# A decoder's two LSTMs: gate sums in three PSUM tiles, half steps written out by hand, and inputs added as three bf16 numbers

## The chip, the core and the metric

The kernel runs on one core of one Trainium2 chip. The metric is the device time of one launch in microseconds (us); lower is better. TensorE is called PE, VectorE DVE, ScalarE ACT, GpSimd POOL and SyncE SP, as the profile does.

## The reference, cut to what matters

The reference is a decoder of four layers with three sublayers each, over 8 sequences of 112 tokens of width 256. The change touches one part of the first sublayer only: the two LSTMs that make its queries and keys. Everything else of the decoder is the same in both kernels.

```python
xW = jnp.einsum('bsd,gd->sbg', x, Wih) + b          # inputs, all steps at once
def step(carry, xt):
    h, c = carry
    gates = xt + h @ Whh.T                          # 8 x 1024, h is 8 x 256
    i, f, g, o = jnp.split(gates, 4, axis=-1)
    c = sigmoid(f) * c + sigmoid(i) * tanh(g)
    h = sigmoid(o) * tanh(c)
    return ((h, c), h)
hq = _lstm(hidden_states, Wih_q, Whh_q, b_q)        # 112 steps
hk = _lstm(hidden_states, Wih_k, Whh_k, b_k)        # 112 steps, independent of hq
```

Each LSTM is a chain of 112 steps in which a step needs the `h` of the step before. The two LSTMs (called chain 0 and chain 1 below) do not need each other. All arithmetic is float32.

## The kernel before, in words

`l0_attn` normalises and transposes the tokens (`ln_T_mm`), runs `lstm`, projects the values (`vv`, line 553) and then attends (`l0_attend`). `xs` keeps the transposed tokens for the LSTMs; it is grouped so that 16 steps of 8 sequences (a block `m` of 128 tokens, seven blocks in all) lie together.

**Layout of a step.** The 1024 gate sums of a chain are spread over four groups `j` of 256 columns, and group `j` is written to PSUM partitions 32j to 32j+31, of which 8 (the sequences) carry numbers. So one tile `g` of 128 x 256 holds all gates of one step, in the order i, f, o, g, 64 columns each, and every ACT and DVE operation on the gates works on 128 partitions.

**PE work of a step.** `from_inputs` (line 609) starts the sums of a step: four matmuls, one for each `j`, whose stationary operand `pick` chooses the 8 rows of step `t` out of the block's 128 rows of `xw`. The recurrent product (line 631) adds `h @ Whh`: two halves `c` of the hidden state by four `j`, 8 matmuls of 256 columns, with the transposed state `hT` (128 x 32, of which 8 columns carry numbers) as the stationary operand. A float32 matmul appears in the trace as two records, and as two weight loads.

**ACT and DVE work of a step.** A sigmoid over 192 columns (line 642), a tanh over 64 (line 643), then on DVE c·f, i·g and their sum (lines 648, 650, 651), tanh of the cell on ACT (line 653), `h` on DVE (line 655), and DVE's transposition in blocks of 32 x 32 into `hT` (line 657). POOL copies `hT` to `hs` for the attention (line 658).

**Inputs.** `inputs` (lines 597 to 604) projects one block of 16 steps for one chain and 512 of its columns: two float32 matmuls of 512 columns with 128 x 128 weights, and a bias add on DVE that writes `xw`. Four such calls stand ahead of the first step; the other 24 are made one after every fourth step (`if t % 4 == 2 and later`).

**What sets the order.** Both chains are written in one loop over `t`, chain 0 and then chain 1. Nothing in the order is by hand: a scheduler orders each engine's instructions, and each engine runs its own in order. The tiles `g0`, `g1` have two PSUM buffers each.

Of the kernel before, what the change touches and what calls it, by code (L numbers as in the profile page):

```python
# [90 lines left out]
def _gates(w):  # L91

    i, f, g, o = np.split(w, 4, axis=0)
    a = np.stack([i, f, o, g]).reshape(4, 2, 4, 32, *w.shape[1:])
    return np.moveaxis(a, 2, 0).reshape(1024, *w.shape[1:])


# [155 lines left out]
def _constants():  # L253

    f32 = np.float32
    i = np.arange(S)
    le = (i[:, None] <= i[None, :]).astype(f32)
    d = i[:, None] - i[None, :]
    k = np.where(np.abs(d) <= 3, np.exp(-(d.astype(f32) ** 2) / f32(2.0 * 0.4**2)), 0).astype(f32)
    local = k / (k.sum(axis=-1, keepdims=True) + f32(1e-10))  # L260
    inv = (1.0 / 10000.0 ** (np.arange(0, 128, 2, dtype=f32) / f32(128))).astype(f32)
    ang = np.outer(inv, i.astype(f32)).astype(f32)
    cos, sin = np.cos(ang), np.sin(ang)

    pick = np.zeros((P, 16, 32), f32)
    for r in range(16):
        pick[16 * np.arange(8) + r, r, np.arange(8)] = 1

    sums = (np.arange(P)[:, None] == 32 * np.arange(4)[None, :] + 16).astype(f32)
    return [  # L270
        ("ident", np.eye(P, dtype=f32)),
        ("causal", np.where(le.T > 0, f32(0), f32(NEG))),
        ("le", le),
        ("gt", 1 - le),
        ("localT", f32(1.0 - 0.6) * local.T),
        ("cos", np.concatenate([cos, cos])),
        ("sin", np.concatenate([sin, -sin])),
        ("ones", np.ones((S, S), f32)),
        ("pick", pick.reshape(P, 512)),
        ("sums", sums),  # L280
        ("first", np.broadcast_to(np.arange(8, 0, -1, dtype=f32)[None], (P, 8))),
    ]
# [65 lines left out]
class _Kernel:  # L348
# [187 lines left out]
    def l0_attn(self):  # L536
        nc, tc, w = self.nc, self.tc, self.w
        with ExitStack() as outer:
            keep = outer.enter_context(tc.tile_pool(name="l0a", bufs=1))
            hs = self.t(keep, [P, S, 2, 2, NB], "hs")  # L540
            vv = self.t(keep, [P, NB, 4, 65], "vv")
            with tc.tile_pool(name="ps_l0a", bufs=2, space=PSUM) as ps:
                xs = self.t(keep, [P, 2, S // 16, NB, 16], "xs")
# [12 lines left out]
            self.l0_attend(hs, vv)  # L556
        w.done("l0a_bv")

    def ln_T_mm(self, ps, xs):

        self.normalise(self.x, self.xn)
        for half in range(2):
            for kc in range(2):
                tp = self.t(ps, [P, 512], "mm")
                for j in range(HB):
                    self.nc.tensor.transpose(
                        tp[:, j * S : (j + 1) * S],
                        self.xn[:S, half * HB + j, kc * P : (kc + 1) * P],
                        self.ident[:S, :S],
                    )  # L570
                bs = slice(half * HB, (half + 1) * HB)
                self.nc.vector.tensor_copy(
                    xs[:, kc, :, bs, :].rearrange("p m b r -> p b m r"),
                    tp[:, :HT].rearrange("p (b m r) -> p b m r", b=HB, r=16),
                )
                self.nc.scalar.copy(self.xnT[:, kc, half * HT : (half + 1) * HT], tp[:, :HT])

    def lstm(self, hs, xs, ps0):
# [4 lines left out]

        nc, tc = self.nc, self.tc
        G = range(4)
        whh = [self.w("l0a_hh_q", 2), self.w("l0a_hh_k", 2)]
        wih = [self.w("l0a_ih_q", 2), self.w("l0a_ih_k", 2)]
        bias = [self.w("l0a_b_q"), self.w("l0a_b_k")]  # L590
        pick = self.c("pick").rearrange("p (r m) -> p r m", r=16)
        with tc.tile_pool(name="ps_lstm", bufs=2, space=PSUM) as ps, tc.tile_pool(
            name="lstm", bufs=2
        ) as work, tc.tile_pool(name="lstm_c", bufs=1) as cpool:

            xw = self.t(cpool, [P, 2, S // 16, 1024], "xw")
            cell = [self.t(cpool, [P, 64], f"cell{l}") for l in range(2)]

            def inputs(m, l, half):
                cols = slice(512 * half, 512 * half + 512)  # L600
                pm = self.t(ps0, [P, 512], "mm")
                steps = [xs[:, k, m, :, :].rearrange("p b r -> p (b r)") for k in range(2)]
                self.mm(pm, [(x, wih[l][:, k, cols]) for k, x in enumerate(steps)])
                nc.vector.tensor_tensor(xw[:, l, m, cols], pm, bias[l][:, cols], ALU.add)

            def from_inputs(t, l):
                g = self.t(ps, [P, 256], f"g{l}")
                for j in G:
                    nc.tensor.matmul(  # L609
                        g[32 * j : 32 * j + 32, :],  # L610
                        pick[:, t % 16, :],
                        xw[:, l, t // 16, 256 * j : 256 * j + 256],
                        start=True,
                        stop=t == 0,
                        skip_group_check=True,
                    )
                return g

            for l in range(2):
                for half in range(2):  # L620
                    inputs(0, l, half)
            later = [(m, l, half) for m in range(1, S // 16) for l in range(2) for half in range(2)]
            gs = [from_inputs(0, l) for l in range(2)]
            hT = [None, None]
            for t in range(S):
                for l in range(2):
                    g = gs[l]
                    if t > 0:
                        for c in range(2):
                            for j in G:  # L630
                                nc.tensor.matmul(  # L631
                                    g[32 * j : 32 * j + 32, :],
                                    hT[l][:, c, :],
                                    whh[l][:, c, 256 * j : 256 * j + 256],
                                    start=False,
                                    stop=c == 1,
                                    skip_group_check=True,
                                )
                    if t + 1 < S:
                        gs[l] = from_inputs(t + 1, l)  # L640
                    sg = self.t(work, [P, 256], f"sg{l}")
                    nc.scalar.activation(sg[:, :192], g[:, :192], AF.Sigmoid)  # L642
                    nc.scalar.activation(sg[:, 192:], g[:, 192:], AF.Tanh)
                    ig, fg, og, gg = (sg[:, 64 * i : 64 * i + 64] for i in range(4))
                    if t == 0:
                        nc.vector.tensor_tensor(cell[l], ig, gg, ALU.mult)
                    else:
                        nc.vector.tensor_tensor(cell[l], cell[l], fg, ALU.mult)
                        tmp = self.t(work, [P, 64], f"tmp{l}")
                        nc.vector.tensor_tensor(tmp, ig, gg, ALU.mult)  # L650
                        nc.vector.tensor_tensor(cell[l], cell[l], tmp, ALU.add)  # L651
                    th = self.t(work, [P, 64], f"th{l}")
                    nc.scalar.activation(th, cell[l], AF.Tanh)  # L653
                    h = self.t(work, [P, 64], f"h{l}")
                    nc.vector.tensor_tensor(h, og, th, ALU.mult)  # L655
                    hT[l] = self.t(work, [P, 2, 32], f"hT{l}")
                    nc.vector.transpose(hT[l].rearrange("p c b -> p (c b)"), h)  # L657
                    nc.gpsimd.tensor_copy(hs[:, t, l, :, :], hT[l][:, :, :NB])
                if t % 4 == 2 and later:
                    inputs(*later.pop(0))  # L660

    def l0_attend(self, hs, vv):
        nc, tc, w = self.nc, self.tc, self.w
# [1374 lines left out]
```

## Time and profile before

| what | value |
|---|---|
| median of 3 runs (lowest, highest) | 2502.42 us (2501.94, 2503.11) |
| the profiled execution, its own time | 2510.28 us |
| its span in the profile | 2508.5 us |
| mean granted PE clock | 0.93 of full |
| granted PE clock from 20 to 430 us | 1.00 |
| busy over the span: PE, DVE, ACT, POOL | 88%, 58%, 32%, 8% |
| LSTM part in the trace: first `from_inputs`, last `hT` written | 31.45 us, 433.07 us |
| start of the last recurrent product | 429.58 us |

The profiled execution took 7.9 us more than the median of the timed runs; durations below are from it. A line such as `L631 PE MATMUL g<-w,hT 128*32 128x256 f32 x3552 | 237.5, 384` reads: line 631, matmuls with a 128 x 32 stationary operand and a 128 x 256 moving one, 3552 records, busy 237.5 us in all (overlaps counted once), 384 ns for one from start to modelled end. After the second bar stands the idle time before them and what ended it.

### The profile page before, as it was taken

What the parts mean: (1) busy time and instruction counts of PE and PEld (TensorE: products, weight loads), DVE (VectorE), ACT (ScalarE), POOL (GpSimd) and SP (SyncE); (2) the same over time, 40 slices, a digit from 0 to 9 for tenths busy, and PEclk for the clock granted to TensorE, in tenths of its full rate; (3) what the DMA queues carried; (4) which work ended last, traced back from release to release, by engine and by line L of the source; (5) the groups of instructions that cost most, each with busy time, mean ns of one, the idle gap of its engine ahead of it and who ended that gap; (6) DMA issues with size and microseconds to landing.
All of it is one profiled execution on the core that took longest, in us unless ns stands there. A gap on an engine that the chain in (4) does not pass through costs nothing.

```text
span 2508.5 us, 43456 instructions
## 1 busy us (share of the span) xinstructions
PE 2219.0 (88%) x17256; PEld 1347.1 (54%) x17256; DVE 1464.2 (58%) x3879; ACT 795.9 (32%) x1988; POOL 212.8 (8%) x416
## 2 busy tenths in 40 slices
PE   6999999989989889999998887899999999799942
PEld 3444444657655656655666444556555556556622
DVE  4565656555544657763688555767660042667698
ACT  2333333111221245641012222367521111346521
POOL 0111111000001110000111331100000000100000
PEclk9999999786899999999999988899999999799966
DMA  4000001000010000001000001000111000000000
GB/s 182 2 2 2 2 19 61 1 17 1 17 51 1 14 18 2 18 18 42 34 3 35 15 18 59 34 2 1 51 51 50 33 17 1 1 1 2 2 0 15
DMA packets 10730, 56.15 MB, mean 22 GB/s; under 512 B 1833, under 2 KB 3625, under 8 KB 5792
## 3 DMA queue, kind: packets, MB, share of 16 engines
q1 hardware_dynamic: 8304, 44.77, 4.9%
q0 software_dynamic: 2080, 7.07, 0.8%
q8 instruction: 137, 2.24, 0.4%
q10 hardware_dynamic: 144, 1.54, 0.2%
q14 instruction: 65, 0.53, 0.1%
HBM read 52.43 MB, written 0.92 MB: 21 GB/s over the span
## 4 chain that ended last, share of the span: by engine, by line
PE 68%; DVE 21%; issue 5%; ACT 4%; DMA 1%; POOL 1%; DVEq 0%; ACTq 0%; POOLq 0%
PE mm L397 32%; PE tr L1058 6%; PE gu L397 6%; PE g L631 6%; PE sc L397 5%; PE av L1074 3%; PE av L397 3%; DVE rot L1367 1%; ACT sg L642 1%; PE s L397 1%; ACT th L653 1%; DVE hT L657 1%; PE g L609 1%; PE tr L397 1%; DVE h L655 1%
## 5 line engine op out<-in xcount | busy, mean ns | idle before, releaser
L631 PE MATMUL g<-w,hT 128*32 128x256 f32 x3552 | 237.5, 384 | 25.7 <-DVE hT L657 24.4
L397 PE MATMUL mm<-xnT,w 128*128 128x448 f32 x432 | 185.8, 567 | 19.4 <-DVE qT L1370 4.5
L1058 PEld LDWEIGHTS tr<-cst,xe 112*125 112x125 f32 x1152 | 151.3, 188 | 96.2 <-issue 36.9
L1045 DVE TENSOR_REDUCE xnm<-sc 112x1 f32<-112x375 f32 x384 | 184.4, 541 | 28.7 <-PE sc L397 28.0
L1058 PE MATMUL tr<-cst,xe 112*125 112x112 f32 x1152 | 192.7, 289 | 8.6 <-DVE xeT L1066 3.4
L397 PE MATMUL mm<-hT,w 128*128 128x448 f32 x512 | 193.0, 540 | 0.0
L631 PEld LDWEIGHTS g<-w,hT 128*32 128x32 f32 x3552 | 96.0, 109 | 167.0 <-DVE hT L657 124.3
L397 PEld LDWEIGHTS mm<-hT,w 128*128 128x128 f32 x512 | 97.3, 190 | 94.2 <-issue 94.2
L397 PE MATMUL mm<-w,oT 128*112 128x256 f32 x416 | 121.0, 449 | 21.6 <-DVE oT L1547 14.2
L609 PE MATMUL g<-xw,cst 128*32 128x256 f32 x1792 | 138.7, 379 | 0.0
L1066 DVE COPY xeT<-tr 125x336 f32<-125x336 f32 x192 | 97.2, 506 | 69.1 <-PE tr L1058 61.6
L397 PEld LDWEIGHTS mm<-xnT,w 128*128 128x128 f32 x432 | 79.0, 196 | 104.0 <-issue 54.0
L1064 ACT COPY xeT<-tr 125x336 f32<-125x336 f32 x192 | 85.0, 443 | 155.0 <-PE tr L1058 155.0
L397 PE MATMUL mm<-w,hT 128*112 128x256 f32 x576 | 132.3, 389 | 0.2 <-DVE xo L1638 0.2
L1049 ACT ACTIVATE xe<-sc,xnm 112x375 f32<-112x375 f32 x256 | 126.3, 582 | 9.2 <-DVE xnm L1045 9.2
L397 PE MATMUL gu<-xnT,w 128*128 128x448 f32 x320 | 124.4, 544 | 1.7 <-DVE hT L1212 1.2
L397 PEld LDWEIGHTS mm<-w,hT 128*112 128x112 f32 x576 | 103.5, 182 | 27.5 <-issue 4.9
L397 PEld LDWEIGHTS mm<-w,oT 128*112 128x112 f32 x416 | 83.9, 211 | 53.4 <-DVE oT L1547 14.4
L642 ACT ACTIVATE sg<-g 128x192 f32<-128x192 f32 x224 | 73.9, 330 | 105.3 <-PE g L631 93.9
L653 ACT ACTIVATE th<-cell 128x64 f32<-128x64 f32 x224 | 57.4, 256 | 146.8 <-DVE cell L651 146.7
L474 DVE TENSOR_TENSOR x<-mm,x 112x256 f32<-112x256 f32 x64 | 27.0, 422 | 129.8 <-PE mm L397 129.8
L655 DVE TENSOR_TENSOR h<-sg,th 128x64 f32<-128x64 f32 x224 | 50.5, 225 | 84.5 <-ACT th L653 84.5
(381 smaller groups left out, 3755.8 us busy)
## 6 DMA issues: line engine op xcount, KB each, us to landing
w<-in_w SPq DMA_DIRECT2D x33, 1024.0 KB, 4.9
w<-in_w SPq DMA_DIRECT2D x4, 896.0 KB, 11.4
raw<-in_wq POOLq DMA_DIRECT2D x3, 1024.0 KB, 5.1
wi<-in_wint POOLq DMA_DIRECT2D x3, 768.0 KB, 6.0
w<-in_w SPq DMA_DIRECT2D x2, 768.0 KB, 4.2
ctxT<-in_ctxT ACTq DMA_DIRECT2D x1, 1500.0 KB, 8.4
cx<-in_ctx POOLq DMA_DIRECT2D x1, 1500.0 KB, 21.0
w<-in_w SPq DMA_DIRECT2D x2, 512.0 KB, 4.0
```

Of the source, the lines that this page charges most:

```text
L397: self.nc.tensor.matmul(out, lhsT, rhs, start=i == 0, stop=i == len(pairs) - 1)
L609: nc.tensor.matmul(g[32 * j : 32 * j + 32, :], pick[:, t % 16, :], xw[:, l, t // 16, 256 * j : 256 * j + 256], start=True, stop=t == 0, sk ...
L631: nc.tensor.matmul(g[32 * j : 32 * j + 32, :], hT[l][:, c, :], whh[l][:, c, 256 * j : 256 * j + 256], start=False, stop=c == 1, skip_group ...
L642: nc.scalar.activation(sg[:, :192], g[:, :192], AF.Sigmoid)
L653: nc.scalar.activation(th, cell[l], AF.Tanh)
L655: nc.vector.tensor_tensor(h, og, th, ALU.mult)
L1045: nc.vector.tensor_reduce(nm, sc, AX.X, ALU.max, negate=True)
L1049: nc.scalar.activation(e, sc, AF.Exp, bias=nm)
L1058: nc.tensor.transpose(tp[:CH, i * S : (i + 1) * S], e[:, i * CH : (i + 1) * CH], self.ident[:S, :S])
L1064: nc.scalar.copy(eT, src)
L1066: nc.vector.tensor_copy(eT, src)
L1074: nc.tensor.matmul(avs[b][32 * j : 32 * j + 32, c * S : (c + 1) * S], values[b % 2][:CH, i, 4 * c + j, :], eTs[b, c, j][:, i, :], start=i ...
```

## The change

Five things change, all in `lstm` and in what prepares for it.

1. **Gates in three parts.** The gate order becomes g, i, f, o, and a step's sums lie in three PSUM tiles, `ga` (g and i, 128 columns), `gf` (64) and `go` (64), each with one buffer. Each matmul of 256 columns becomes three, of 128, 64 and 64. The activations become one tanh over 64 columns and three sigmoids over 64.
2. **Half steps.** The loop runs over 224 half steps `n` (step `n // 2` of chain `n % 2`), and the order on PE, DVE and ACT is the order of the code (`manual_schedule`). In half step `n` PE runs the recurrent product of its chain, then the other chain's `from_inputs` for half step `n + 1`. ACT runs this chain's tanh, then the other chain's tanh of its cell (`state`), then the three sigmoids.
3. **State.** The cell and the output gate are transposed on their own (`cT`, `oT`), so tanh of the cell and `hT` work on 128 x 16, and `hT` is 128 x 2 x 8: its stationary operand has 8 columns and not 32.
4. **Inputs as three bf16 numbers.** For blocks 1 to 6 a projected input is cut into three bf16 numbers whose sum it is: ACT copies to bf16 and POOL subtracts, twice, and POOL copies the rest. Twelve DMAs from SBUF to SBUF for each block and chain (144 in all, 32 partitions by 1024 columns each) bring the three numbers of a token under each other (rows 0-31, 32-63, 64-95 of `moved`). `from_inputs` then multiplies by `add3` (96 x 32, bf16), which chooses and adds the three. Block 0 stays float32.
5. **Projection 64 columns a time.** A generator, `inputs`, makes 128 columns of a block in five stages, of which one is run in each half step (two in each of the first 16): 64 columns, 64 columns and the bias add, then the three cuts. 96 such generators run; from half step 16 on a new one starts at every even `n`, the last at `n` = 174. Half steps 176 to 223 have no projection.

Two small parts: `pick` and `xs` are laid out with the step ahead of the sequence, and three DVE copies make `add3` at the start.

```diff
-    a = np.stack([i, f, o, g]).reshape(4, 2, 4, 32, *w.shape[1:])
+    a = np.stack([g, i, f, o]).reshape(4, 2, 4, 32, *w.shape[1:])
...
-        pick[16 * np.arange(8) + r, r, np.arange(8)] = 1
+        pick[8 * r + np.arange(8), r, np.arange(8)] = 1
...
+            add3 = self.t(cpool, [P, 4, 32], "add3", BF16)
+            for i in range(3):
+                nc.vector.tensor_copy(add3[32 * i : 32 * i + 32], pick[:32, :4, :])
...
+            def inputs(m, l, q):
+                cols = slice(128 * q, 128 * q + 128)
+                pm = self.t(ps0, [P, 512], "mm")[:, :128]
+                for i in range(2):
+                    projected(pm[:, 64 * i : 64 * i + 64], m, l, slice(128 * q + 64 * i, 128 * q + 64 * i + 64))
+                    if i == 0:
+                        yield
+                x = self.t(work, [P, 128], "x")
+                nc.vector.tensor_tensor(x, pm, bias[l][:, cols], ALU.add)
...
+                for i in range(3):
+                    yield
+                    part = cuts[l][:, i, cols]
+                    if i == 2:
+                        nc.gpsimd.tensor_copy(part, x)
+                    else:
+                        nc.scalar.copy(part, x)
+                        nc.gpsimd.tensor_tensor(x, x, part, ALU.subtract)
+                if q == 7:
+                    moved[m, l] = self.t(work, [P, 4, 1024], f"xm{l}", BF16)
+                    for i in range(3):
+                        for r in range(4):
+                            nc.sync.dma_start(
+                                moved[m, l][32 * i : 32 * i + 32, r, :], cuts[l][32 * r : 32 * r + 32, i, :]
+                            )
+            def product(g, lhsT, rhs, l, part, start, stop):
+                at, n = PARTS[part]
                 for j in G:
                     nc.tensor.matmul(
+                        g[32 * j : 32 * j + lhsT.shape[1], :], lhsT, rhs[:, 256 * j + at : 256 * j + at + n],
+                        start=start, stop=stop, skip_group_check=True,
                     )
...
+                    if m == 0:
+                        product(g, pick[:, r, :], first[l], l, part, True, t == 0)
+                    else:
+                        product(g, add3[:96, r % 4, :], moved[m, l][:96, r // 4, :], l, part, True, False)
...
+            def state(t, l):
+                cT, oT = turned[l]
+                th = self.t(work, [P, 2, NB], f"th{l}")
+                nc.scalar.activation(th, cT[:, :, :NB], AF.Tanh)
+                hT[l] = self.t(work, [P, 2, NB], f"hT{l}")
+                nc.vector.tensor_tensor(hT[l], oT[:, :, :NB], th, ALU.mult)
+                nc.gpsimd.tensor_copy(hs[:, t, l, :, :], hT[l])
+            with tc.manual_schedule(engines={ET.PE, ET.DVE, ET.Activation}):
+                gs = [from_inputs(0, 0), None]
+                for n in range(2 * S):
+                    t, l = n // 2, n % 2
                     if t > 0:
+                        for part, g in enumerate(gs[l]):
+                            for c in range(2):
+                                product(g, hT[l][:, c, :], whh[l][:, c, :], l, part, False, c == 1)
+                    ga, gf, go = gs[l]
+                    if n + 1 < 2 * S:
+                        gs[1 - l] = from_inputs((n + 1) // 2, 1 - l)
...
+                    nc.scalar.activation(flat[:, :64], ga[:, :64], AF.Tanh)
+                    if n > 0:
+                        state((n - 1) // 2, 1 - l)
+                    nc.scalar.activation(flat[:, 64:128], ga[:, 64:], AF.Sigmoid)
+                    tmp = self.t(work, [P, 64], f"tmp{l}") if t > 0 else cell[l]
+                    nc.vector.tensor_tensor(tmp, ig, gg, ALU.mult)
+                    nc.scalar.activation(flat[:, 128:192], gf, AF.Sigmoid)
+                    nc.scalar.activation(flat[:, 192:], go, AF.Sigmoid)
+                    if t > 0:
                         nc.vector.tensor_tensor(cell[l], cell[l], fg, ALU.mult)
                         nc.vector.tensor_tensor(cell[l], cell[l], tmp, ALU.add)
+                    turned[l] = [self.t(work, [P, 2, 32], f"{i}T{l}") for i in "co"]
+                    nc.vector.transpose(turned[l][0].rearrange("p c b -> p (c b)"), cell[l])
+                    nc.vector.transpose(turned[l][1].rearrange("p c b -> p (c b)"), og)
+                    for i in range(2 if n < 16 else 1):
+                        running = [r for r in running if next(r, r) is not r]
+                        if later and (i == 0 if n < 16 else n % 2 == 0):
+                            running.append(inputs(*later.pop(0)))
+                            next(running[-1])
+                state(S - 1, 1)
```

More of the change, by code (lines that the diff above doesn't have):

```diff
@@ L542, in l0_attn @@
             with tc.tile_pool(name="ps_l0a", bufs=2, space=PSUM) as ps:
-                xs = self.t(keep, [P, 2, S // 16, NB, 16], "xs")
+                xs = self.t(keep, [P, 2, S // 16, 16, NB], "xs")
                 self.ln_T_mm(ps, xs)
@@ L572, in ln_T_mm @@
                 self.nc.vector.tensor_copy(
-                    xs[:, kc, :, bs, :].rearrange("p m b r -> p b m r"),
+                    xs[:, kc, :, :, bs].rearrange("p m r b -> p b m r"),
                     tp[:, :HT].rearrange("p (b m r) -> p b m r", b=HB, r=16),
@@ L587, in lstm @@
         G = range(4)
+        PARTS = ((0, 128), (128, 64), (192, 64))
         whh = [self.w("l0a_hh_q", 2), self.w("l0a_hh_k", 2)]
@@ L590, in lstm @@
         bias = [self.w("l0a_b_q"), self.w("l0a_b_k")]
-        pick = self.c("pick").rearrange("p (r m) -> p r m", r=16)
-        with tc.tile_pool(name="ps_lstm", bufs=2, space=PSUM) as ps, tc.tile_pool(
+        with tc.tile_pool(name="ps_lstm", bufs=1, space=PSUM) as ps, tc.tile_pool(
             name="lstm", bufs=2
         ) as work, tc.tile_pool(name="lstm_c", bufs=1) as cpool:
-            xw = self.t(cpool, [P, 2, S // 16, 1024], "xw")
+            pick = self.c("pick").rearrange("p (r m) -> p r m", r=16)
+            add3 = self.t(cpool, [P, 4, 32], "add3", BF16)
+            for i in range(3):
+                nc.vector.tensor_copy(add3[32 * i : 32 * i + 32], pick[:32, :4, :])
@@ L597, in lstm, with projected @@
             cell = [self.t(cpool, [P, 64], f"cell{l}") for l in range(2)]
[L599 to L602, printed above, removed]
+            first = [self.t(cpool, [P, 1024], f"xw{l}") for l in range(2)]
+            cuts, moved = {}, {}
+            def projected(pm, m, l, cols):
+                steps = [xs[:, k, m, :, :].rearrange("p r b -> p (r b)") for k in range(2)]
@@ L603, in inputs @@
                 self.mm(pm, [(x, wih[l][:, k, cols]) for k, x in enumerate(steps)])
-                nc.vector.tensor_tensor(xw[:, l, m, cols], pm, bias[l][:, cols], ALU.add)
-            def from_inputs(t, l):
-                g = self.t(ps, [P, 256], f"g{l}")
+            def inputs(m, l, q):
[7 more added lines that the diff above has]
+                nc.vector.tensor_tensor(x, pm, bias[l][:, cols], ALU.add)
+                if q == 0:
+                    cuts[l] = self.t(cpool, [P, 3, 1024], f"xc{l}", BF16)
+                for i in range(3):
[13 more added lines that the diff above has]
+                            )
@@ L608, in from_inputs @@
+            def product(g, lhsT, rhs, l, part, start, stop):
+                at, n = PARTS[part]
                 for j in G:
                     nc.tensor.matmul(
[L610 to L615, printed above, removed]
-                    )
-                return g
+                        g[32 * j : 32 * j + lhsT.shape[1], :], lhsT, rhs[:, 256 * j + at : 256 * j + at + n],
+                        start=start, stop=stop, skip_group_check=True,
+                    )
@@ new lines, in from_inputs @@
+            def from_inputs(t, l):
+                gs = [self.t(ps, [P, 512], f"g{l}{part}")[:, :n] for part, (_, n) in enumerate(PARTS)]
+                m, r = t // 16, t % 16
+                for part, g in enumerate(gs):
+                    if m == 0:
+                        product(g, pick[:, r, :], first[l], l, part, True, t == 0)
+                    else:
+                        product(g, add3[:96, r % 4, :], moved[m, l][:96, r // 4, :], l, part, True, False)
+                return gs
@@ L619, in lstm @@
             for l in range(2):
                 for half in range(2):
[L621 to L627, printed above, removed]
-                    if t > 0:
[L629 to L647, printed above, removed]
@@ new lines, in lstm @@
+                    cols = slice(512 * half, 512 * half + 512)
+                    pm = self.t(ps0, [P, 512], "mm")
+                    projected(pm, 0, l, cols)
+                    nc.vector.tensor_tensor(first[l][:, cols], pm, bias[l][:, cols], ALU.add)
+            later = [(m, l, q) for m in range(1, S // 16) for l in range(2) for q in range(8)]
+            running = []
+            hT, turned = [None, None], [None, None]
+            def state(t, l):
[5 more added lines that the diff above has]
+                nc.gpsimd.tensor_copy(hs[:, t, l, :, :], hT[l])
@@ new lines, in lstm @@
+            with tc.manual_schedule(engines={ET.PE, ET.DVE, ET.Activation}):
+                gs = [from_inputs(0, 0), None]
+                for n in range(2 * S):
+                    t, l = n // 2, n % 2
+                    if t > 0:
+                        for part, g in enumerate(gs[l]):
[4 more added lines that the diff above has]
+                        gs[1 - l] = from_inputs((n + 1) // 2, 1 - l)
+                    sg = self.t(work, [P, 4, 64], f"sg{l}")
+                    flat = sg.rearrange("p g u -> p (g u)")
+                    gg, ig, fg, og = (sg[:, i, :] for i in range(4))
+                    nc.scalar.activation(flat[:, :64], ga[:, :64], AF.Tanh)
[7 more added lines that the diff above has]
+                    if t > 0:
@@ L648, in lstm @@
                         nc.vector.tensor_tensor(cell[l], cell[l], fg, ALU.mult)
-                        tmp = self.t(work, [P, 64], f"tmp{l}")
-                        nc.vector.tensor_tensor(tmp, ig, gg, ALU.mult)
                         nc.vector.tensor_tensor(cell[l], cell[l], tmp, ALU.add)
[L652 to L660, printed above, removed]
+                    turned[l] = [self.t(work, [P, 2, 32], f"{i}T{l}") for i in "co"]
+                    nc.vector.transpose(turned[l][0].rearrange("p c b -> p (c b)"), cell[l])
+                    nc.vector.transpose(turned[l][1].rearrange("p c b -> p (c b)"), og)
```

## The prediction

> **What bounds the kernel now.** I read the costliest groups first, for the share of the LSTM part, then the timeline of one step, to see what a step waits for, then the timeline around one input projection. The groups (line, engine, operation, shape, count, busy us, mean ns of one, idle before):
>
> ```profile
> L631 PE MATMUL g<-w,hT 128*32 128x256 f32 x3552 | 237.5, 384 | 25.7 <-DVE hT L657 24.4
> L609 PE MATMUL g<-xw,cst 128*32 128x256 f32 x1792 | 138.7, 379 | 0.0
> L642 ACT ACTIVATE sg<-g 128x192 f32<-128x192 f32 x224 | 73.9, 330 | 105.3 <-PE g L631 93.9
> ```
>
> PE looks full, yet it waits for `hT`, and ACT waits for PE: the two are on one chain. The timeline of 408 to 412 us (start, duration, engine, line) follows one chain through a step:
>
> ```profile
> 408.23 1.07 PE L631 MATMUL g<-w,hT 128*32 128x256 f32 x16
> ...
> 409.42 0.33 ACT L642 ACTIVATE sg<-g 128x192 f32<-128x192 f32 x1 [0.16 <-PE g L631]
> ...
> 409.93 0.22 DVE L650 TENSOR_TENSOR tmp<-sg 128x64 f32<-128x64 f32 x1
> ...
> 410.18 0.23 DVE L651 TENSOR_TENSOR cell<-cell,tmp 128x64 f32<-128x64 f32 x1
> ...
> 410.50 0.26 ACT L653 ACTIVATE th<-cell 128x64 f32<-128x64 f32 x1 [0.63 <-DVE cell L651]
> ...
> 410.79 0.23 DVE L655 TENSOR_TENSOR h<-sg,th 128x64 f32<-128x64 f32 x1 [0.38 <-ACT th L653]
> ...
> 411.45 1.07 PE L631 MATMUL g<-w,hT 128*32 128x256 f32 x16
> ```
>
> From 408.23 to 411.45 is 3.22 us, and this is the period of a step nearly everywhere: the latency of PE, ACT, DVE, ACT, DVE in turn, 1.61 us for each half step. PE's own work is less. Sixteen records of 384 ns end within 1.07 us because the four column groups run side by side: records start 6 to 7 ns apart in fours, and fours follow each other by 216 ns. So a product costs 4 x 0.216 = 0.86 us of PE, `from_inputs` 0.43, both chains 2.6 us of 3.22. Every fourth step a projection comes in:
>
> ```profile
> 199.54 0.62 PE L609 MATMUL g<-xw,cst 128*32 128x256 f32 x8
> ...
> 200.09 1.98 PE L397 MATMUL mm<-w,xs 128*128 128x512 f32 x4
> ...
> 202.00 0.59 PEld L631 LDWEIGHTS g<-w,hT 128*32 128x32 f32 x16 [0.76 <-DVE hT L657]
> ```
>
> That step takes 4.80 us, 1.58 more: 24 x 1.58 = 38 us. 112 x 3.22 + 38 = 399 us, and the trace has 401.6 from the first `from_inputs` to the last `hT`.
>
> **What the Trainium skill says.** TensorEngine Tiling (Array Packing), Key Properties: a change of tiling mode drains TensorE. The trace agrees: the last four of L609 start at 199.78 and stream 0.213, the 128-column weights load at 200.09; the last L397 starts at 201.48 and streams 0.427, the next load is at 202.00. Both gaps are 0.095 us. TensorE: Matmul & The Clock Gate, LDWEIGHTS: a load takes its columns over 1.2 GHz; here 128-column float32 loads follow each other by 0.107 us, and at 112 columns short matmuls (65 columns wide) come every 0.098: the load bounds them. Its section Back-to-back issue gap has a floor of about 25 ns between matmuls; between column groups this trace has 6 to 7. SBUF — State Buffer, section SBUF: two separate sides: GpSimd and a VectorE operation with two SBUF inputs exclude each other. The trace agrees: line 1410 on DVE takes 407 ns alone and 941 beside POOL.
>
> **The change, part by part.** The changed program's order on PE is as written: 24 matmuls of the product, 12 of the other chain's `from_inputs`, then the projection's two.
>
> *Product.* Per 4 groups, 4 rounds of 128 columns and 8 of 64. By the width (216 ns for 256, 95.5 for 112 in the `av` matmuls of line 1074, also with 32-column loads) a round of 128 is 0.109, one of 64 is 0.0555. With 0.02 to start: 0.90 us, as before. Rounds of 64 columns in column groups are not in the trace. Below: 0.0555, the stream itself, as the load has 8 columns and not 32. Above: 0.11, if a load's latency (110 ns for L631's) no longer hides behind so short a round. I take the lower end, as loads there start 29 ns after those before them.
>
> *`from_inputs`, bf16.* One pass: 0.055, and twice 0.035 for 64 columns (stream 0.027, a load of 32 columns about the same): 0.125 us, against 0.43. A change of type alone costs nothing where bf16 transposes follow float32 matmuls (line 1925: 0.055 apart at once). Above: three times 0.11.
>
> *Projection.* Two matmuls, four records of 64 columns, bounded by the loads: drain 0.095, first to second 0.204 (two loads in line), twice 0.112, stream 0.053, drain 0.095: 0.67 us in each half step up to 175. Both drains are new here: two per half step, where before two came per four steps.
>
> So PE needs 0.90 + 0.125 + 0.67 = 1.70 us per half step while there is projection.
>
> *Chain.* Product start to the semaphore of `ga` 0.68 (last round at 0.37, 0.27 to its end, 0.04), ACT starts at 0.76 (0.08, as before), the other chain's tanh 0.12 behind and 0.23 long, DVE's `hT` at 1.17 for 0.18, PE 0.04 later: 1.40. The long way round (sigmoid i, tmp, cell, transposition, cT at 2.2, tanh in the next half step at 0.88) asks for the same 1.4. DVE's own waits: 1.42. So a half step is bounded by this chain at **1.42 us** without projection, by PE at **1.70** with it; before it was 1.61 + 38/224 = 1.78.
>
> *ACT, DVE, POOL, SP.* Beside these: a 128-column ACT copy per half step (about 0.29, from 0.44 at 336 columns), a DVE bias add every second (0.29, from 0.42 at 256), POOL's subtraction per half step (about 0.53, from 1.13 at 448 and 0.77 at 256) and copies. Each engine stays under 1.3 us of 1.70. They are queued after the sigmoids and transpositions; who waits behind the copy is the next tanh, due 0.7 us later. POOL holds up DVE where they meet: I take 2 us in all. The 144 DMAs sit on SP alone; the weight loads behind them are needed only later, and each block has 13 half steps (over 20 us) to land: nothing.
>
> *Sum.* Half steps 0 and 1: 4 us. 2 to 15, with float32 `from_inputs` (0.44) and eight projection records: 0.90 + 0.44 + 0.095 + 0.204 + 6 x 0.112 + 0.053 + 0.095 = 2.46, x14 = 34.4. 16 to 31: 2.01 x16 = 32.2. 32 to 175: 1.70 x144 = 244.8. 176 to 222: 1.42 x47 = 66.7. Together 382.1 us to the last product's start, where the trace has 429.58 - 31.45 = 398.1: 16 less. The three copies for `add3` stand on DVE in the first normalisation: +0.4. The value projections that fill PE after the last product do so in both. With POOL: **14 us less**. The profiled execution took 2510.28, so about 2496; from the median of 2502.42 it is **2488 us**.
>
> **Rivals.**
> - *Small rounds do not pack* (slower). If a round of 64 costs more than its stream, PE pays it in every half step. Decides from 0.08 us per half step, 10 ns a round (14 us over 176). At 0.075 a round and 0.06 in bf16: +0.22 x176 = 39 us, 2527. At 0.11 everywhere: half steps of 2.35 with and 1.67 without projection, +125 us, 2613. For it: no such narrow round is in the trace, and 128 PE instructions never took less than 1.89 us there, when I ask 1.70 for about 130. Against it: bursts of 32 go out in 0.31 us. Chance 0.2.
> - *A new wait on POOL or ACT* (same or slower): subtraction against the cell's operations, then the in-order ACT copy ahead of the next tanh. +0.1 us in 144 half steps gives 2502, +0.2 gives 2517. For it: 941 against 407 ns. Against: POOL starts when the cell's sum is already running. Chance 0.15.
> - *PE has more room* (faster): the drains fall partly into waits, and the chain's 1.42 to 1.5 holds throughout. -0.2 to -0.28 x144: 2448 to 2459. For it: the chain, not PE, bounded the old loop. Against: both drains are measured. Chance 0.15.
> - That the change does not do what it says is excluded by the order of its instructions.
>
> **How the numbers follow.** The forecast (2475 to 2500) has 0.5. A measurement of this kernel can tell about 0.2%, 5 us, from no change. Faster by more: 0.45 of the forecast's 0.5, all 0.15 of more room, 0.02 of the rest, 0.62. Within 0.2%: 0.04, and 0.07 from the two slower rivals, 0.11. Slower: 0.27. The range 2450 to 2532 leaves out the full failure to pack and half of the best case.
>
> **What would show it.** Right: half steps of 1.7 us up to about 175 with PE without gaps, 1.4 after it, rounds of 64 columns 55 ns apart, 0.095 us around each projection. Wrong: product records of 64 columns 75 ns apart or more, PE idle ahead of a product while projections run, DVE cell operations of 0.4 us, or a half step over 1.78.

## The result, and the profile after

The changed kernel takes **2529.11 us** (median of 4 runs, 2523.32 to 2531.38); the kernel before took 2502.59 beside it. The ratio is 1.0107, 95% interval 1.0094 to 1.0119: about 1.1% **slower**, where 0.6% faster was forecast. The value lies in the range of 2450 to 2532 us, but the direction is wrong.

The profiled execution took 2531.38 us, with a span of 2529.6, 21.1 more than before. In it the LSTM stage, from the first write of `hT` to the last, takes 424.6 us (35.35 to 459.91) against 399.0 (33.86 to 432.82): +25.6. The first write is 1.5 later, and everything after the last one takes 2069.7 us against 2075.7. So the stage holds the loss. From its costliest groups:

```profile
L647 PE MATMUL g<-w,hT 128*8 128x64 f32 (+1 forms) x10656 | 242.7, 237 | 21.5 <-issue 12.1
L647 PEld LDWEIGHTS g<-w,hT 128*8 128x8 f32 x10656 | 199.3, 89 | 41.7 <-issue 16.4
L695 ACT ACTIVATE sg<-g 128x64 f32<-128x64 f32 x224 | 50.2, 224 | 222.1 <-PE g L647 222.1
```

The product was 3552 records waiting for `hT`; it is 10,656 now, and most of its idle time ends at "issue": PE stood still, and the profile shows nothing that it waited for. ACT's first operation of a half step, the tanh of line 695, waits for PE alone. The timeline of PE over five half steps with projection (start, duration, engine, line, operation, records, idle before):

```profile
199.90 0.66 PE L397 MATMUL mm<-w,xs 128*128 128x64 f32 x4
200.49 1.07 PE L647 MATMUL g<-w,hT 128*8 128x128 f32 x48
201.38 0.29 PE L647 MATMUL g<-xm,add 96*32 96x128 bf16 x11
202.07 0.20 PE L647 MATMUL g<-xm,add 96*32 96x64 bf16 x1 [0.40 <-issue]
202.20 0.66 PE L397 MATMUL mm<-w,xs 128*128 128x64 f32 x4
202.79 1.07 PE L647 MATMUL g<-w,hT 128*8 128x128 f32 x48
203.68 0.30 PE L647 MATMUL g<-xm,add 96*32 96x128 bf16 x12
203.91 0.66 PE L397 MATMUL mm<-w,xs 128*128 128x64 f32 x4
204.49 1.07 PE L647 MATMUL g<-w,hT 128*8 128x128 f32 x48
205.38 0.62 PE L647 MATMUL g<-xm,add 96*32 96x128 bf16 x12
205.93 0.66 PE L397 MATMUL mm<-w,xs 128*128 128x64 f32 x4
```

The half step from 202.79 to 204.49 takes 1.70 us, the predicted figure. Its neighbours take 2.30 and 2.03, and each loses the difference in one place: between the eleventh and twelfth of twelve matmuls that have no new operand to wait for (201.38 to 202.07), and again inside 205.38 + 0.62. Between 110 and 310 us about every third half step has such a pause, of 0.3 to 0.9 us from one start to the next. After half step 176 it is about every second, mostly with 0.4 to 1.4 us (one has 2.95).

What keeps such a pace is found in the DMA queues. Queue q8, of the kind "instruction", brings packets of 16,384 bytes. From 110 to 310 us before, then after (queue, packets, MB, share of 16 engines):

```profile
q8 instruction: 21, 0.34, 0.8%
```

```profile
q8 instruction: 54, 0.88, 1.9%
```

In the same 200 us PE has 5,403 records (matmuls and weight loads) before and 13,838 after, which is 257 and 256 for each packet. So these packets carry PE's program, and one holds 256 instructions, 64 bytes each. In the kernel before one came every 9.5 us; now one comes every 3.7.

### The profile page after: what moved, and what is told of

The parts are those of the page before. It is cut to its first block, busy times and chain, and to the rows that moved or that the text cites. A ratio compares the mean times of both kernels' runs of the same rounds, so it can differ in the third digit from the quotient of the medians.

```text
span 2529.6 us, 62844 instructions
## 1 busy us (share of the span) xinstructions
PE 2227.6 (88%) x26312; PEld 1519.3 (60%) x26312; DVE 1485.1 (59%) x4178; ACT 834.2 (33%) x2629; POOL 340.8 (13%) x704
## 3 DMA queue, kind: packets, MB, share of 16 engines
q10 hardware_dynamic: 144, 1.54, 0.2%
## 4 chain that ended last, share of the span: by engine, by line
PE 74%; DVE 16%; issue 5%; ACT 3%; DMA 1%; POOL 1%; DVEq 0%; ACTq 0%; POOLq 0%
PE mm L397 35%; PE g L647 10%; PE gu L397 6%; PE tr L1113 6%; PE sc L397 5%; PE av L1129 3%; PE av L397 3%; DVE rot L1422 1%; PE s L397 1%; PE tr L397 1%; DMA cx<-in_ctx 1%; PE tr L496 1%; PE tr L520 1%; DVE xnm L1100 1%; DVE xn L435 1%
## 5 line engine op out<-in xcount | busy, mean ns | idle before, releaser
L647 PE MATMUL g<-w,hT 128*8 128x64 f32 (+1 forms) x10656 | 242.7, 237 | 21.5 <-issue 12.1
L647 PEld LDWEIGHTS g<-w,hT 128*8 128x8 f32 x10656 | 199.3, 89 | 41.7 <-issue 16.4
L397 PE MATMUL mm<-w,xs 128*128 128x64 f32 (+1 forms) x784 | 134.3, 296 | 3.6 <-issue 2.1
L695 ACT ACTIVATE sg<-g 128x64 f32<-128x64 f32 x224 | 50.2, 224 | 222.1 <-PE g L647 222.1
L678 DVE TENSOR_TENSOR hT<-oT,th 128x16 f32<-128x16 f32 x224 | 39.3, 176 | 138.4 <-ACT th L676 135.9
L397 PEld LDWEIGHTS mm<-w,xs 128*128 128x128 f32 x784 | 103.5, 191 | 20.2 <-issue 9.0
```

Source lines behind the costliest of these rows:

```text
L397: self.nc.tensor.matmul(out, lhsT, rhs, start=i == 0, stop=i == len(pairs) - 1)
L647: nc.tensor.matmul(g[32 * j : 32 * j + lhsT.shape[1], :], lhsT, rhs[:, 256 * j + at : 256 * j + at + n], start=start, stop=stop, skip_grou ...
L678: nc.vector.tensor_tensor(hT[l], oT[:, :, :NB], th, ALU.mult)
L695: nc.scalar.activation(flat[:, :64], ga[:, :64], AF.Tanh)
```

## Theories

- **A, instruction supply.** PE gets 256 instructions in no less than about 3.6 us, 14 ns each. A half step now has 128 (product 48 loads and 48 matmuls, inputs 12 and 12, projection 4 and 4), or 120 without projection, where the kernel before had about 49. All else in the prediction holds.
- **B, narrow rounds.** The 64-column rounds cost more than their stream.
- **C, another wait.** POOL, ACT's order, or the 144 moves.

## The experiments

All times are medians; the ratio is to the kernel before on the same chip, with its 95% interval. Half steps are mean intervals between writes of `hT`: "with" from half step 32 to 175, "without" from 177 to 222. Packets are those of queue q8 from 110 to 310 us. "Stage" is the time from the first write of `hT` to the last. Half steps, packets and stages are read from one profiled execution of each kernel.

| kernel | PE instructions in a half step, with projection | with, us | without, us | packets | stage, us | ratio |
|---|---|---|---|---|---|---|
| before | 49 | 1.81 | 1.69 | 21 | 399.0 | 1 |
| after | 128 | 1.86 | 1.80 | 54 | 424.6 | 1.0107 |
| e1 two parts | 88 | 1.69 | 1.45 | 40 | 381.5 | 0.9942 (0.9927 to 0.9957) |
| e2 four parts | 168 | 2.43 | 2.30 | 54 | 549.4 | 1.0582 (1.0566 to 1.0598) |
| e3 before, split | 145 | 2.09 | 2.12 | 55 | 465.9 | 1.0272 (1.0255 to 1.0290) |
| e4 projection of 128 | 124 | 1.78 | 1.75 | 55 | 404.7 | 1.0053 (1.0033 to 1.0073) |
| e5 two parts and 128 | 84 | 1.54 | 1.40 | 43 | 347.6 | 0.9798 (0.9771 to 0.9824) |

The packets tell it shortest: four different kernels, of 124 to 168 instructions a half step, all stop at 54 or 55 packets in 200 us, one in 3.64 to 3.70 us. The three that need fewer get fewer.

### e1: two parts in place of three

```diff
-        PARTS = ((0, 128), (128, 64), (192, 64))
+        PARTS = ((0, 128), (128, 128))
...
-                    ga, gf, go = gs[l]
+                    ga, gfo = gs[l]
...
-                    nc.scalar.activation(flat[:, 128:192], gf, AF.Sigmoid)
-                    nc.scalar.activation(flat[:, 192:], go, AF.Sigmoid)
+                    nc.scalar.activation(flat[:, 128:192], gfo[:, :64], AF.Sigmoid)
+                    nc.scalar.activation(flat[:, 192:], gfo[:, 64:], AF.Sigmoid)
```

> The changed kernel with two parts of the gates in place of three: f and o share one tile of 128 columns, so a half step has 16 rounds of four 128-column matmuls, as weight loads and matmuls 32 + 32 in the product, 8 + 8 in the inputs, 4 + 4 in the projection, 88 in place of 132; columns streamed, sigmoids and everything on the other engines stay. Instruction supply (TensorE gets at most 256 instructions in about 3.5 us, some 14 ns each): 88 x 14 = 1.2 us is under the chain of a half step, the pauses inside the products go, half steps while projecting come to 1.65 to 1.75 us and to 1.4 to 1.5 after that, the whole to 2480 to 2495 us, 35 to 50 below the changed kernel. Narrow rounds that do not pack: the 64-column rounds are gone as well, so a gain of the same size, but the pauses of the changed kernel would then be inside its 64-column rounds only. Waits on POOL, ACT or the 144 moves: nothing changes, 2520 to 2535 us.

Measured: 2494.21 us beside 2507.48. POOL, ACT, DVE and the moves have the same work as in the changed kernel, so C falls as the cause of its loss. PE's timeline shows half steps alike, 1.69 us, and no pause:

```profile
199.86 1.06 PE L647 MATMUL g<-w,hT 128*8 128x128 f32 x32
200.73 0.30 PE L647 MATMUL g<-xm,add 96*32 96x128 bf16 x8
200.96 0.66 PE L397 MATMUL mm<-w,xs 128*128 128x64 f32 x4
201.55 1.06 PE L647 MATMUL g<-w,hT 128*8 128x128 f32 x32
202.42 0.30 PE L647 MATMUL g<-xm,add 96*32 96x128 bf16 x8
202.65 0.66 PE L397 MATMUL mm<-w,xs 128*128 128x64 f32 x4
203.24 1.06 PE L647 MATMUL g<-w,hT 128*8 128x128 f32 x32
```

The product fills the same 0.87 to 0.89 us with 32 matmuls as with 48: the columns set it, not the number of rounds. B is not excluded by this run alone, since the narrow rounds went too.

### e2: the wide matmuls split as well

```diff
-                for j in G:
-                    nc.tensor.matmul(
-                        g[32 * j : 32 * j + lhsT.shape[1], :], lhsT, rhs[:, 256 * j + at : 256 * j + at + n],
-                        start=start, stop=stop, skip_group_check=True,
-                    )
+                for s in range(0, n, 64):
+                    for j in G:
+                        nc.tensor.matmul(
+                            g[32 * j : 32 * j + lhsT.shape[1], s : s + 64],
+                            lhsT, rhs[:, 256 * j + at + s : 256 * j + at + s + 64],
+                            start=start, stop=stop, skip_group_check=True,
+                        )
```

> The changed kernel with each 128-column matmul of the product and of the inputs issued as two of 64 columns into the same tile: the same columns streamed, the same tiles, waits and order on every engine, 168 TensorE instructions in a half step with projection in place of 132, 160 without in place of 120. Instruction supply: 168 x 14 ns = 2.35 us and 160 x 14 = 2.2 us a half step in place of 1.86 and 1.79, so some 0.45 us x 200 = 80 to 100 us more, 2605 to 2630 us. Columns alone (a round of 64 costs half of one of 128): no change, 2525 to 2540 us. Narrow rounds that do not pack: slower too, by an amount that the spacing of rounds in the trace gives.

Measured: 2653.24 us. Against the changed kernel that is 0.0475 x 2502 = 119 us, more than the 80 to 100 expected: the first 32 half steps, which I had left out, lose too (2.90 and 2.81 us against 2.48 and 2.15), and an instruction costs 14.5 ns, not 14. PE runs, and stops inside the product:

```profile
200.32 0.28 PE L648 MATMUL g<-w,hT 128*8 128x64 f32 x5
201.18 1.01 PE L648 MATMUL g<-w,hT 128*8 128x64 f32 x58 [0.57 <-issue]
...
202.88 0.89 PE L648 MATMUL g<-w,hT 128*8 128x64 f32 x49
204.90 0.35 PE L648 MATMUL g<-w,hT 128*8 128x64 f32 x12 [1.14 <-issue]
```

Between the pauses 58 matmuls take 0.79 us (201.18 to 201.97), 13.6 ns each, the 0.055 us that I took for a round of four. So B falls here: narrow rounds pack, until PE has nothing more to run. The changed kernel shows it as well: in its half step at 202.79 the eight 64-column rounds start 0.056 us apart.

### e3: the old kernel with more instructions

```diff
+                            for at, n in PARTS:
                                 for j in G:
                                     nc.tensor.matmul(
-                                        g[32 * j : 32 * j + 32, :],
+                                        g[32 * j : 32 * j + 32, at : at + n],
                                         hT[l][:, c, :],
-                                        whh[l][:, c, 256 * j : 256 * j + 256],
+                                        whh[l][:, c, 256 * j + at : 256 * j + at + n],
```

and the same for `from_inputs`.

> The kernel before with each 256-column matmul of the product and of the inputs issued as three, of 128, 64 and 64 columns, into the same tile: the same columns, waits and order, no half steps reordered, no cut into bf16, no moves; 144 TensorE instructions in a half step in place of 48. Instruction supply: 144 x 14 ns = 2.0 us a half step in place of 1.61, so 70 to 100 us slower than the kernel before, 2575 to 2605 us. Columns alone: 2500 to 2515 us. If the changed kernel was slow by its POOL work, its moves or its order of ACT, this kernel would not be slow.

Measured: 2575.77 us; 0.0272 x 2502 = 68 us over the kernel before, just under the 70 expected. It has none of the new order, cuts or moves, and it gets the same pauses. Its groups:

```profile
L634 PE MATMUL g<-w,hT 128*32 128x64 f32 (+1 forms) x10656 | 268.1, 239 | 50.0 <-issue 31.6
...
L611 PE MATMUL g<-xw,cst 128*32 128x64 f32 (+1 forms) x5376 | 163.2, 238 | 28.2 <-issue 28.2
```

The number of instructions is enough to slow a kernel whose columns and waits are untouched.

### e4: projection of 128 columns in every second half step

```diff
-                for i in range(2):
-                    projected(pm[:, 64 * i : 64 * i + 64], m, l, slice(128 * q + 64 * i, 128 * q + 64 * i + 64))
-                    if i == 0:
-                        yield
+                projected(pm, m, l, cols)
+                yield
```

> The changed kernel with its three parts, but the projection of 128 columns done in one stage in every second half step in place of 64 in each: 248 TensorE instructions in a pair of half steps in place of 264, two changes of tiling fewer (2 x 0.095 us). Instruction supply: 248 x 14 ns = 3.47 us a pair in place of 3.72, so 0.12 us a half step over 144 half steps, about 15 to 20 us less, 2508 to 2515 us. Were the stream and the changes of tiling what bounds it: 1.59 us a half step in place of 1.86, 35 to 40 us less, 2488 to 2495. A wait on POOL or ACT: no change.

Measured: 2518.60 us. On the base of the first comparison, 1.0053 x 2502.6 = 2516, just above what A expected (2508 to 2515). Half of the changes of tiling are gone, yet the half step is not at 1.59 but at 1.78, and 124 x 3.64 / 256 is 1.76: with three parts PE's supply sets the half step, so the projection saves only what its four instructions fewer are worth.

### e5: both

The edits of e1 and e4 together.

> Both cuts of the instruction count together: two parts of the gates, and the projection of 128 columns done in one stage of every second half step. 160 TensorE instructions in a pair of half steps, 2.3 us at 14.4 ns: the supply is far from binding. Then what the prediction summed decides: a half step at the chain's 1.42 us followed by one at 1.75 of TensorE work, 1.59 us on average in place of 1.69 in the kernel with two parts alone (143 half steps, 15 us less), and about 0.35 us less in the first 15: 2470 to 2480 where the kernel before takes 2505, a ratio of 0.985 to 0.990. If something else than the changes of tiling and the stream holds the half step at 1.69, the ratio stays at 0.994.

Measured: 2451.50 us beside 2502.47, **2.0% faster than the kernel before** (interval 1.8% to 2.3%) and 3.1% below the changed one. The half step is 1.54 us, below the 1.59 of the working, and the first 31 gain as well (2.06 us from 1 to 15, 1.70 after). PE now waits for `hT` in the half step without projection, as it should:

```profile
199.76 1.06 PE L645 MATMUL g<-w,hT 128*8 128x128 f32 x32
200.64 0.30 PE L645 MATMUL g<-xm,add 96*32 96x128 bf16 x8
201.10 1.06 PE L645 MATMUL g<-w,hT 128*8 128x128 f32 x32 [0.17 <-DVE hT L676]
201.98 0.30 PE L645 MATMUL g<-xm,add 96*32 96x128 bf16 x8
202.21 0.71 PE L397 MATMUL mm<-w,xs 128*128 128x128 f32 x4
202.85 1.06 PE L645 MATMUL g<-w,hT 128*8 128x128 f32 x32
```

A projection of 128 columns takes 0.64 us to the next product (202.21 to 202.85), one of 64 took 0.59. What does not depend on the columns (four loads of weights and the changes of tiling) is nearly all of it, so half as many projections cost little more than half. The working had a pair at 1.42 + 1.75; the trace has 1.34 + 1.75.

### e6: the supply by itself

```diff
+            for n in (8, 64, 128, 256):
+                g = self.t(ps, [P, 256], "g0")
+                for i in range(200):
+                    for j in G:
+                        nc.tensor.matmul(
+                            g[32 * j : 32 * j + 32, :n], hT[1][:, 0, :],
+                            whh[1][:, 0, 256 * j : 256 * j + n],
+                            start=True, stop=True, skip_group_check=True,
+                        )
```

> The kernel before, with four stretches of matmuls added after the LSTMs that nothing waits for and whose results are not used: 200 rounds over the four column groups at 8 columns, then 200 each at 64, 128 and 256 (800 matmuls and 800 weight loads a stretch, 6.25 fetches of 256 instructions). Instruction supply: the stretch of 8 columns takes as long as that of 64, both about 1,600 x 14.3 ns = 23 us once the first fetches are used up; the one of 128 columns (0.109 us a round) about the same, 22 to 24 us; only that of 256 is set by its columns, 200 x 0.215 = 43 us. Columns or weight loads as the only limit: 8 columns 2 to 10 us, 64 columns 11 us, 128 columns 22 us, 256 columns 43 us.

A float32 matmul is two records, so a stretch has 1600 matmuls and 1600 loads, twice what I wrote, and all the times expected double. Measured: 44.2 us at 8 columns, 44.4 at 64, 45.5 at 128, 86.5 at 256. At 8 and 64 columns this is A's order: eight times the columns, the same time. At 128 the run does not tell the two apart, since 200 rounds of two records, 0.109 us each, are 43.6 us by the columns alone and PE shows no pauses there; at 256 the columns set it. The timeline, two bursts at 8 columns and three at 64, shows why:

```profile
443.13 1.90 PE L665 MATMUL g<-w,hT 128*32 128x8 f32 x128 [1.83 <-issue]
446.86 1.89 PE L665 MATMUL g<-w,hT 128*32 128x8 f32 x128 [1.83 <-issue]
...
490.00 1.99 PE L665 MATMUL g<-w,hT 128*32 128x64 f32 x128 [1.47 <-issue]
493.73 1.99 PE L665 MATMUL g<-w,hT 128*32 128x64 f32 x128 [1.74 <-issue]
497.19 1.99 PE L665 MATMUL g<-w,hT 128*32 128x64 f32 x128 [1.47 <-issue]
```

Once a stretch is under way, 128 matmuls go out with their 128 loads, 256 instructions, and then comes a pause of 1.5 to 1.8 us; a new burst starts mostly every 3.46 or 3.73 us. A burst goes out in 1.7 us (first to last start), 6.6 ns an instruction; with the pauses it costs 14. The granted clock was 0.56 in the first stretch and 0.90 in the second, so it is not the clock that makes them equal. In a cycle at 8 columns the packet's transfer starts 1.1 us after PE resumes and takes 1.3, and PE resumes 2.6 us after its start. What fills the other 1.3 us no view shows.

### e7: one sigmoid for f and o

```diff
-                    nc.scalar.activation(flat[:, 128:192], gfo[:, :64], AF.Sigmoid)
-                    nc.scalar.activation(flat[:, 192:], gfo[:, 64:], AF.Sigmoid)
+                    nc.scalar.activation(flat[:, 128:], gfo, AF.Sigmoid)
```

> The kernel with two parts and 128-column projections, with one sigmoid over f and o (128 columns) in place of two of 64. ACT loses 0.15 to 0.2 us in each half step. If ACT is off the path, and only the wait for f's half counts, the longer sigmoid puts 0.03 to 0.08 us on the chain of each half step, 5 to 15 us slower than its twin. If ACT's order is on the path, 0 to 10 us faster.

Measured: 2458.43 us, ratio 0.9830 (0.9802 to 0.9858). The intervals of the twins overlap, so the totals don't separate them; the stage does: 1.59 us a half step against 1.54, 355.0 us against 347.6. The trace names a cause that the expectation left out. In e5 the sum of the cell on DVE starts just ahead of POOL's subtraction, here just behind it. First e5, then e7:

```profile
204.51 0.22 DVE L703 TENSOR_TENSOR cell<-cell,tmp 128x64 f32<-128x64 f32 x1
204.58 0.44 POOL L633 TENSOR_TENSOR x<-x,xc 128x128 f32<-128x128 f32 x1 [0.19 <-ACT xc L632]
```

```profile
203.28 0.43 POOL L633 TENSOR_TENSOR x<-x,xc 128x128 f32<-128x128 f32 x1
203.31 0.47 DVE L702 TENSOR_TENSOR cell<-cell,tmp 128x64 f32<-128x64 f32 x1
```

This is so from 110 to 310 us throughout: POOL is first in all 126 half steps of e7, and the sum takes 0.47 us; DVE is first in all 129 of e5, and the sum takes 0.22. The delay is on the path: in 124 of the 126 half steps the tanh of the cell starts 0.03 us after `cT` is done, where in e5 it keeps its 0.12 us behind the tanh of g. So the edit turned the order of DVE and POOL round; by which step it did so, and what a later f or a shorter ACT would be worth without that, this run does not show. In the half steps after 176, which have no subtraction, the medians of e5 and e7 are both 1.40 us.

### e8: the gates in one part

`PARTS = ((0, 256),)`, and the five activations read slices of one tile.

> The changed kernel with the gates in one part: each matmul 256 columns, one tile, 16 + 16 TensorE instructions in a product in place of 48 + 48 (some 48 in a half step with projection), the five activations in the same order but none before the whole product is done. Instruction supply is then no limit, but tanh of g, tanh of the other chain and sigmoid of i no longer lie beside the product: 3 x 0.224 = 0.67 us of ACT, of which 0.45 lay beside it, comes onto the chain: 1.85 to 1.95 us a half step with and without projection, the whole 2520 to 2550 us. If the split hides less than that, as little as 2495.

Measured: 2507.24 us, ratio 1.0010 (1.0000 to 1.0020); half steps of 1.78 us with projection and 1.83 without, a stage of 411.8. ACT gets nothing before the whole product is done:

```profile
201.61 0.22 ACT L695 ACTIVATE sg<-g 128x64 f32<-128x64 f32 x1 [0.91 <-PE g L647]
```

So splitting is worth 411.8 - 381.5 = 30 us of the stage when it is done in two parts, and minus 13 in three. (e1 and e8 ran on two chips; the kernel before takes 2507.48 us on the one and 2502.47 on the other.) The half steps are 0.02 to 0.07 us below the lower end of my expectation, and the total is lower still: what follows the last `hT` took 2059 us in this run, against 2076 before. Over the profiled runs (e6 apart, whose added work falls there) that remainder, which no edit touches, lies between 2059 and 2076 at granted clocks of 0.930 to 0.937; the cause stays open, and stages are compared where a few microseconds matter.

## Why the prediction was wrong, point by point

- **The PE sum as a count of streams, loads and drains: right.** The changed kernel has 1.70 us in the half step at 202.79, and with the supply out of the way (e1) the mean is 1.69. In that half step the product takes 0.89 us (0.90 predicted), `from_inputs` with the drain behind it 0.23 (0.125 + 0.095), the rest of the projection 0.58 (0.575). Inside the projection two terms are off and cancel: its second record starts 0.16 us after the first, not 0.204, and the next product 0.20 after its last record, not 0.053 + 0.095. The drain ahead of the projection, for which the prediction cites the Trainium skill, TensorEngine Tiling (Array Packing), Key Properties, is there in e1 too: the last round of `from_inputs` starts at 202.504 and streams 0.055 us, the projection's first load starts at 202.650, a gap of 0.09. Half steps 2 to 15: 2.46 predicted, 2.48 in the changed kernel; 16 to 31: 2.01, and 2.00 in e1.
- **The chain, 1.42 us: right as a latency.** Undisturbed half steps after 176 take 1.40 in the changed kernel; means are 1.45 in e1, 1.40 in e5.
- **POOL's 2 us and the moves at nothing: no sign against them in this kernel.** From 110 to 310 us POOL's subtraction starts behind the cell's sum in all 108 half steps, as the prediction expected, and the sum takes 0.22 us. e1 keeps subtraction and moves and reaches 0.9942, which on the base of 2502.42 is 2488 us, the forecast. But the small price hung on who starts first, by 0.07 us; e7 has the other order and pays in every half step. The reading behind it, "407 ns alone", is not quite what the old trace has: that operation met the last 0.13 us of one of POOL's, and the seven of about 941 ns met 0.66 us.
- **The step that failed is "PE needs 0.90 + 0.125 + 0.67 = 1.70 us".** It counts streams, loads and drains, and gives the number of instructions no price. 49 in a half step became 128, and 128 x 3.7 / 256 is 1.85 us: the supply, not the stream, is the longest of PE's limits. The bound of 1.42 us after half step 175 fails by the same omission: there 120 instructions ask for 120 x 3.7 / 256 = 1.73 us, and 1.80 was measured. Over the half steps the missing term is (1.86 - 1.70) x 143 = 23 us with projection, (1.80 - 1.42) x 46 = 17 without, and (2.15 - 2.01) x 16 = 2 ahead of them: 42, where forecast and result differ by 41.
- **The text had the clue and set it aside.** "128 PE instructions never took less than 1.89 us" in the old trace stood against narrow rounds, with "bursts of 32 go out in 0.31 us" as the answer. A burst shorter than 256 instructions says what PE can run, not what it is given; e6 shows 256 of them going out in 1.7 us and then nothing for as long. The old trace could not show the limit itself: nowhere in it do 256 PE instructions in a row go out in less than 8.1 us.
- **The rival "small rounds do not pack" gave 2527 us**, nearly the result, for another reason; that the range, drawn wide enough for it, holds the result is luck. Its sign, rounds of 64 columns 75 ns apart, is absent (56 ns), and so are cell operations of 0.4 us from 110 to 310 us. A half step over 1.78 came true (1.86). PE stood idle while projections ran, but inside its runs of matmuls, where the prediction had looked ahead of a product.

## What to carry to other kernels

Count the instructions that an edit gives an engine, weight loads included, and divide the time of the stage by them: on PE here, a plan that asks for less than about 14 ns each over many times 256 of them was not met, whatever its columns. It shows as idle time that ends at "issue" between like instructions, and as instruction packets at a steady shortest interval. Splitting work so that a follower can start early is paid for in instructions: two parts gained 30 us of this stage, three lost more than that again. And a small edit can turn round which of two engines starts first: in e7 0.07 us ahead became 0.04 us behind, and the sum took 0.25 us longer.

## What the runs showed of the hardware

Here PE's instructions came in packets of 256 (16,384 bytes), over longer stretches one per 3.5 to 3.7 us at best, while PE ran such a packet in 1.7 us (e6). The limit was the same, 54 or 55 packets in 200 us, with SBUF-to-SBUF moves running (the changed kernel) and without (e3), and e6 has it at granted clocks of 0.56 and 0.90. Why a packet takes that long stays open. A change of tiling and the weights around it cost nearly as much for a projection of 64 columns (0.59 us) as for one of 128 (0.64). A DVE sum of two SBUF operands that started 0.04 us behind a POOL subtraction took 0.47 us, one that started 0.07 us ahead of it 0.22 (e7, e5).
